# A graph layer's neighbour sum on one core: engine orders written out by hand, two-part float32r rows of 2 KB, and sets of three groups

## The chip, the core and the metric

The kernel runs on one core of a Trainium2 chip. A core has five engines with queues of their own: TensorE (PE, matrix products; PEld is its loading of weights), VectorE (DVE), ScalarE (ACT), GpSimd (POOL) and SyncE (SP). DMA transfers are issued from the queues of POOL, ACT and SP. The metric is the device time of one execution in microseconds (us). Each number of the profile comes from one execution under the hardware profiler.

## What is computed

x has 12500 rows of 256 values, float32. There are 200000 edges with random `src` and sorted `dst`.

```python
h   = relu(layernorm(x))                         # per row
agg = segment_sum(h[src], dst, num_segments=12500)
z   = (1.0 + eps_gin) * h + agg
t   = relu(batchnorm(z @ W1 + b1, g1, bt1))      # W1: 256 x 512
y   = t @ W2 + b2                                # W2: 512 x 256
out = x + relu(batchnorm(y + h, g2, bt2))
```

The batch norms take mean and variance over all 12500 rows, so the first needs every row of `z @ W1`, and the second every row of `y + h`.

## The kernel before

**Tiles.** Nodes are cut into 25 chunks of 512 (`NCH`, `CH`), edges into 1563 tiles of 128, tiles into 131 groups of 12 (`GT`, `NG`). As `dst` is sorted, the edges of a tile reach few nodes; all of a group's nodes lie in a window of `WIDE` = 128 + 2 x `MARGIN` = 280 nodes that moves by `STEP` = 96 nodes per group. A look at the indices ahead (flag L207) picks `fast()` or a general way; with these inputs it is `fast()`.

**A group's work (stage 1).** `gather` (L378 to L387) issues 12 indirect DMAs on POOL (L383), each of which fetches 128 rows by the indices in `srcT` into a buffer `gt`. The pool of these buffers has `AHEAD + 1` = 5, and the loop issues the gather of group i + 4 while it works on group i, so that it needs the buffer of group i - 1. `sums` (L404) makes 12 one-hot matrices of 128 x 128 in one VectorE instruction (L408) and has TensorE multiply and add up the 12 tiles in PSUM (L418): sums by place in a tile's node range. `join` (L423) copies the sums to SBUF on ScalarE (`zs`, L425) and makes the placing matrix `at` (L427); `put` (L432) multiplies both (`pz`, L437), which turns the sums and moves them to their place in the window; `add` (L442) adds the window to the chunk(s) of z that it touches (`zc`, L450). A chunk of z is loaded by `z_chunk` from `h_cols`, the transposed h, and scaled by 1 + eps (L397). When the window has passed a chunk, `first_layer` (L453) multiplies it by W1 in four slices of 128 outputs (L459), takes each slice's statistics (L463) and a copy (L464), and stores all four by one DMA of 1 MB (L465) into `t_tab`.

**The lead-in.** h is made from x by `h_chunk` (L355): `settle` (L323) takes statistics on VectorE (bn_stats L329, over two rows at once), the root on ScalarE (L334), the reciprocal (L336) and the offset (L338) on VectorE, and four relus on ScalarE (L340); the chunk is stored in the table `h_tab` (ACT's queue), transposed on TensorE (L366), copied (L370 on ScalarE, L372 on VectorE) and stored in `h_cols` (SP's queue, L373). Until the table is complete, gathers can't read it. So the first `LEAD` = 24 groups fetch rows of x itself, and `settle` makes h of them in place: 6 bn_stats and 12 relus for a group. `h_chunk` runs in the same iterations.

**Stages 2 and 3** (L510 to L559) read `t_tab` and `h_cols`, multiply by W2, keep `y + h` in SBUF, and after the second statistics transpose back, add x and store.

**What sets the order.** A planner in the language's library orders each engine's instructions; the written order is only a guide to it. In the trace of before it puts, for example, two matmuls of the next group's `sums` ahead of a group's `pz`. Waits between engines follow from the data and the buffers.

Of the kernel before, what the change touches and what calls it, by code (L numbers as in the profile page):

```python
# [7 lines left out]
F32 = mybir.dt.float32  # L8
I32 = mybir.dt.int32
AF = mybir.ActivationFunctionType  # L10
OP = mybir.AluOpType
# [4 lines left out]
R = 4  # L16
EPS = 1e-5
GT = 12
MARGIN = 76
AHEAD = 4  # L20
LEAD = 24
# [9 lines left out]
def kernel(  # L31
# [233 lines left out]
    def fast():  # L265
# [24 lines left out]
        with ExitStack() as fs:  # L290
# [7 lines left out]

            with ExitStack() as es:
                ln = es.enter_context(tc.tile_pool(name="ln", bufs=2))  # L300
                gat = es.enter_context(tc.tile_pool(name="gat", bufs=AHEAD + 1))
                sel = es.enter_context(tc.tile_pool(name="sel", bufs=2))
                zcp = es.enter_context(tc.tile_pool(name="zc", bufs=4))
                tsp = es.enter_context(tc.tile_pool(name="ts", bufs=2))
                ps_h = es.enter_context(tc.tile_pool(name="ps_h", bufs=1, space=PSUM))
                ps_i = es.enter_context(tc.tile_pool(name="ps_i", bufs=1, space=PSUM))
                ps_s = es.enter_context(tc.tile_pool(name="ps_s", bufs=2, space=PSUM))
                ps_z = es.enter_context(tc.tile_pool(name="ps_z", bufs=1, space=PSUM))
                ps_t = es.enter_context(tc.tile_pool(name="ps_t2", bufs=2, space=PSUM))
# [3 lines left out]
                col = ps_i.tile([P, WIDE], F32, name="col")  # L313
# [30 lines left out]
                xts = {}  # L344

                def x_chunk(g):
                    if g >= NCH:
                        return
                    n = chunks[g][1] * R
                    xts[g] = ln.tile([P, R, D], F32, name="xt", bufs=4)  # L350
                    if n < CH:
                        nc.vector.memset(xts[g], 0.0)
                    carry(nc.sync, xts[g], x, g, store=False)

                def h_chunk(g):  # L355
                    n = chunks[g][1] * R
                    slots = len(parts[g])
                    x_chunk(g + 2)
                    ht = ln.tile([P, R, D], F32, name="ht")
                    settle(xts.pop(g), -(-slots // 2), slots, ht, "c")  # L360
                    carry(nc.scalar, ht, h_tab, g, store=True)
                    hc = ln.tile([P, DC, CH], F32, name="hc")
                    for d in range(DC):
                        ph = ps_h.tile([P, CH], F32, name="pc")
                        for c in range(slots):
                            nc.tensor.transpose(  # L366
                                ph[:, c * P : (c + 1) * P], ht[:, c, d * P : (d + 1) * P], ident
                            )
                        if d % 2:
                            nc.scalar.copy(hc[:, d, :n], ph[:, :n])  # L370
                        else:
                            nc.vector.tensor_copy(hc[:, d, :n], ph[:, :n])  # L372
                    nc.sync.dma_start(h_cols[g, :, :, :n], hc[:, :, :n])  # L373

                groups = [(t0, min(GT, NTILE - t0)) for t0 in range(0, NTILE, GT)]
                gathered = {}

                def gather(i):  # L378
                    t0, n = groups[i]
                    ga = gat.tile([P, GT, D], F32, name="gt")  # L380
                    for t in reversed(range(t0, t0 + n)):
                        rows = left if t == full_tiles else P
                        nc.gpsimd.indirect_dma_start(  # L383
                            out=ga[:rows, t - t0, :], out_offset=None, in_=x if i < LEAD else h_tab,
                            in_offset=bass.IndirectOffsetOnAxis(ap=srcT[:rows, t : t + 1], axis=0),
                        )
                    gathered[i] = ga  # L387

                zc = {}

                def z_chunk(c):
                    if c in zc or c >= NCH:
                        return
                    n = chunks[c][1] * R
                    zc[c] = zcp.tile([P, DC, CH], F32, name="zc")
                    nc.sync.dma_start(zc[c][:, :, :n], h_cols[c, :, :, :n])
                    nc.scalar.activation(zc[c][:, :, :n], zc[c][:, :, :n], AF.Copy, scale=gin1)  # L397
# [4 lines left out]
                summed, placed = {}, {}  # L402

                def sums(i):  # L404

                    t0, n = groups[i]
                    oh = sel.tile([P, GT, P], F32, name="oh")
                    nc.vector.tensor_tensor(  # L408
                        oh[:, :n, :],
                        col[:, :P].unsqueeze(1).to_broadcast([P, n, P]),  # L410
                        dstT[:, t0 : t0 + n].unsqueeze(2).to_broadcast([P, n, P]),
                        op=OP.is_equal,
                    )
                    ga = gathered.pop(i)
                    ps = ps_s.tile([P, D], F32, name="ps")
                    for j in range(n):
                        rows = left if t0 + j == full_tiles else P
                        nc.tensor.matmul(  # L418
                            ps, lhsT=oh[:rows, j, :], rhs=ga[:rows, j, :], start=(j == 0), stop=(j == n - 1)
                        )  # L420
                    summed[i] = ps

                def join(i):  # L423
                    zs = sel.tile([P, D], F32, name="zs", bufs=3)
                    nc.scalar.copy(zs, summed.pop(i))  # L425
                    at = sel.tile([P, WIDE], F32, name="at")
                    nc.vector.tensor_scalar(  # L427
                        at, col, shift[:, i : i + 1], None, op0=OP.is_equal
                    )
                    placed[i] = zs, at  # L430

                def put(i):  # L432

                    zs, at = placed.pop(i)
                    pz = ps_z.tile([P, DC, CH], F32, name="pz2")
                    for d in range(DC):
                        nc.tensor.matmul(  # L437
                            pz[:, d, :WIDE], lhsT=zs[:, d * P : (d + 1) * P], rhs=at, start=True, stop=True
                        )
                    return pz  # L440

                def add(i, pz):  # L442
                    lo, hi = span(i)
                    for c in range(max(lo, 0) // CH, -(-min(hi, N) // CH)):
                        z_chunk(c)
                        a, b = max(lo, c * CH, 0), min(hi, (c + 1) * CH, N)
                        if a >= b:
                            continue
                        side = zc[c][:, :, a - c * CH : b - c * CH]
                        nc.vector.tensor_add(side, pz[:, :, a - lo : b - lo], side)  # L450
                    z_chunk(max(lo, 0) // CH + 1)

                def first_layer(c):  # L453
                    n = chunks[c][1] * R
                    ts = tsp.tile([P, HC, CH], F32, name="ts")
                    for f in range(HC):
                        ph = ps_t.tile([P, CH], F32, name="ph")
                        for d in range(DC):
                            nc.tensor.matmul(  # L459
                                ph[:, :n], lhsT=w1s[:, d, f * P : (f + 1) * P],  # L460
                                rhs=zc[c][:, d, :n], start=(d == 0), stop=(d == DC - 1),
                            )
                        nc.vector.bn_stats(st1[:, f, c, :], ph[:, :n])  # L463
                        nc.scalar.copy(ts[:, f, :n], ph[:, :n])  # L464
                    nc.scalar.dma_start(t_tab[c, :, :, :n], ts[:, :, :n])  # L465
                    del zc[c]

                x_chunk(0)
                x_chunk(1)
                for i in range(min(AHEAD, NG)):  # L470
                    gather(i)
                made = done = 0
                for i in range(NG + 1):

                    while made < NCH and made < 2 + NCH * i // (LEAD - AHEAD):
                        h_chunk(made)
                        made += 1
                    if i + AHEAD < NG:
                        gather(i + AHEAD)
                    pz = None  # L480
                    if i > 0:
                        join(i - 1)
                        pz = put(i - 1)
                    if i < NG:
                        if i < LEAD:
                            settle(gathered[i], GT // 2, GT, gathered[i], "g")
                        sums(i)
                    if i == 0:
                        continue
                    add(i - 1, pz)  # L490
                    nxt = span(i)[0] if i < NG else N
                    while done < NCH and min((done + 1) * CH, N) <= nxt:
                        first_layer(done)
                        done += 1
# [316 lines left out]
```

## Time and profile before

| what | value |
|---|---|
| median of 3 runs | 2267.43 us (2265.9 to 2267.68) |
| the profiled execution | 2627.44 us |
| its span, first to last instruction | 2625.6 us |
| its mean granted TensorE clock | 0.754 |
| lead-in with gathers of x, 32 to 505 us | POOL 273.97 us busy, DVE 210.53, ACT 218.53, PE 226.22; DMA share 0.55 |
| gathers of the table, 505 to 2328 us | POOL 1208.69, DVE 372.33, ACT 125.46, PE 922.82; DMA share 0.36 |
| to the start of stage 2, 2328 to 2378 us | PE 37.18, POOL 0 |
| stage 2, 2378 to 2548 us | PE 170.00 |
| stage 3, 2548 to 2626 us | PE 40.86; DMA share 0.77 |

The profiled execution is 360 us longer than the median; all rows below the second are of it. A line of the profile's groups has line, engine, operation, out<-in by the program's names and a count; then busy time in all and the mean of one in ns; then the idle time of the engine just before these instructions, with what ended most of it. "issue" is idle time in which the engine waited for nothing that the profile shows, "remote" a release that it can't tie to an instruction of this core. A line of the waits has who waited for whom, us in all, how often, the longest. A line of the timeline has start, duration, engine, line, operation, and in brackets the idle time before it.

### The profile page before, as it was taken

To read this page: it belongs to the slowest core of one execution; us is meant where nothing else is said; L and a number is where in the kernel's file an instruction comes from. 1 tells how busy PE (TensorE), PEld (TensorE's weight loads), DVE (VectorE), ACT (ScalarE), POOL (GpSimd) and SP (SyncE) were. 2 spreads that over 40 slices of the span, in tenths; PEclk is the share of its full clock that TensorE was granted. 3 is DMA by queue.
4 is the path that set the end of the run, shared out by engine and by line. 5 is a ranking of instruction groups with operands and counts; after the bars stand their busy time and mean duration, and the time that the engine had idled before them with its cause. 6 is when DMAs were issued, how large, how long until landed. Compare 5 with 4: busy or idle time off the path is not lost.

```text
span 2625.6 us, 14777 instructions
## 1 busy us (share of the span) xinstructions
PE 1404.3 (53%) x4873; PEld 1001.2 (38%) x4873; DVE 716.2 (27%) x1060; ACT 460.3 (18%) x871; POOL 1484.3 (57%) x1575
## 2 busy tenths in 40 slices
PE   1234566645455455445545545544555553578995
PEld 1223344434434334343333424433334442453444
DVE  5234555412212112122111212211121211133444
ACT  1335465510000000000000000000000000013434
POOL 4654656666666666666666666566666666630000
PEclk6666777777777777677777767777777776788996
DMA  5444665433333333333333333333333333328728
GB/s 163 158 152 136 206 199 185 139 114 92 116 119 108 100 120 112 92 116 119 113 92 116 112 94 118 105 120 92 119 110 96 116 114 90 108 77 328 273 82 301
DMA packets 150067, 349.41 MB, mean 133 GB/s; under 512 B 28920, under 2 KB 84366, under 8 KB 143838
## 3 DMA queue, kind: packets, MB, share of 16 engines
q0 software_dynamic: 75008, 204.90, 26.9%
q1 hardware_dynamic: 44182, 91.21, 10.0%
q10 hardware_dynamic: 30792, 52.26, 5.3%
q8 instruction: 41, 0.67, 0.1%
q14 instruction: 44, 0.36, 0.0%
HBM read 284.26 MB, written 64.00 MB: 133 GB/s over the span
## 4 chain that ended last, share of the span: by engine, by line
another core or an unknown queue 50%; PE 25%; issue 10%; ACT 6%; DVE 5%; DMA 3%; POOL 1%; ACTq 0%; SPq 0%; DVEq 0%; POOLq 0%
PE ps L418 9%; PE py L527 6%; PE pz L437 4%; PE ph L459 4%; ACT gt L340 3%; DVE st L463 1%; DMA out_dram<-ot 1%; ACT zs L425 1%; POOL gt L383 1%; ACT ht L340 1%; DVE oh L408 1%; PE po L551 1%; ACT zc L397 1%; DMA zc<-h_cols 1%
## 5 line engine op out<-in xcount | busy, mean ns | idle before, releaser
L383 POOL DMA_INDIRECT gt<-h_tab,srcT x1275 | 1208.9, 948 | 616.4 <-issue 373.8
L418 PE MATMUL ps<-gt,oh 128*128 128x256 f32 x3126 | 767.2, 406 | 88.8 <-ACT gt L340 70.8
L418 PEld LDWEIGHTS ps<-gt,oh 128*128 128x128 f32 x3126 | 648.3, 208 | 206.9 <-ACT gt L340 74.3
L437 PE MATMUL pz<-at,zs 128*128 128x280 f32 x524 | 210.8, 538 | 789.1 <-ACT zs L425 672.0
L408 DVE TENSOR_TENSOR oh<-col,dstT 128x1536 f32<-128x1536 f32 x131 | 229.1, 1749 | 1192.6 <-remote 942.9
L437 PEld LDWEIGHTS pz<-at,zs 128*128 128x128 f32 x524 | 121.6, 248 | 850.2 <-ACT zs L425 693.3
L383 POOL DMA_INDIRECT gt<-in_x_dram,srcT x288 | 273.8, 951 | 196.5 <-ACT zs L425 109.3
L425 ACT COPY zs<-ps 128x256 f32<-128x256 f32 x131 | 48.8, 372 | 1614.0 <-remote 1261.3
L459 PE MATMUL ph<-zc,w1s 128*128 128x512 f32 (+1 forms) x400 | 210.3, 677 | 206.2 <-ACT ts L464 138.2
L459 PEld LDWEIGHTS ph<-zc,w1s 128*128 128x128 f32 x400 | 84.9, 220 | 311.6 <-issue 154.9
L450 DVE TENSOR_TENSOR zc<-pz,zc 128x560 f32<-128x560 f32 (+9 forms) x203 | 100.9, 527 | 315.8 <-remote 189.8
L527 PE MATMUL py<-tT,w2s 128*128 128x512 f32 (+1 forms) x400 | 170.9, 591 | 11.7 <-ACT tT L520 11.7
L340 ACT ACTIVATE gt<-gt,nbg,rsg 128x256 f32<-128x256 f32 x288 | 149.5, 590 | 4.2 <-DVE nbg L338 1.9
L527 PEld LDWEIGHTS py<-tT,w2s 128*128 128x128 f32 x400 | 76.9, 193 | 105.7 <-issue 87.2
L463 DVE BATCH_NORM_STATS2 st<-ph 128x6 f32<-128x512 f32 (+1 forms) x100 | 67.1, 681 | 153.5 <-PE ph L459 60.1
L329 DVE BATCH_NORM_STATS2 stg<-gt 128x6 f32<-128x512 f32 x144 | 91.5, 689 | 34.7 <-DMA gt<-in_x_dram,srcT 22.6
L464 ACT COPY ts<-ph 128x512 f32<-128x512 f32 (+1 forms) x100 | 57.4, 575 | 194.9 <-DVE st L463 150.6
L520 ACT ACTIVATE tT<-ti,of,sc 128x512 f32<-128x512 f32 (+1 forms) x100 | 72.1, 791 | 100.8 <-issue 86.7
L366 PE MATMUL pc<-ident,ht 128*128 128x128 f32 x196 | 38.2, 327 | 66.1 <-issue 27.9
L427 DVE TENSOR_SCALAR at<-col,shift 128x280 f32<-128x280 f32 x131 | 65.5, 500 | 0.3 <-PE pz L437 0.3
L531 DVE TENSOR_TENSOR yT<-py,yT 128x512 f32<-128x512 f32 (+1 forms) x50 | 33.9, 678 | 110.2 <-PE py L527 110.2
L366 PEld LDWEIGHTS pc<-ident,ht 128*128 128x128 f32 x196 | 27.7, 168 | 84.9 <-issue 33.8
(74 smaller groups left out, 393.8 us busy)
## 6 DMA issues: line engine op xcount, KB each, us to landing
t_tab<-ts ACTq DMA_DIRECT2D x24, 1024.0 KB
ti<-t_tab SPq DMA_DIRECT2D x24, 1024.0 KB
gt<-h_tab,srcT POOLq DMA_INDIRECT x1275
xt<-in_x_dram SPq DMA_DIRECT2D x24, 512.0 KB
h_tab<-ht ACTq DMA_DIRECT2D x24, 512.0 KB
h_cols<-hc SPq DMA_DIRECT2D x24, 512.0 KB
zc<-h_cols SPq DMA_DIRECT2D x24, 512.0 KB
yT<-h_cols SPq DMA_DIRECT2D x24, 512.0 KB
```

What stands on the lines that cost most here:

```text
L329: nc.vector.bn_stats(st[:, c : c + 2, :].rearrange("p c s -> p (c s)"), v[:, c : c + 2, :].rearrange("p c d -> p d c"),)
L340: nc.scalar.activation(to[:, c, :], v[:, c, :], AF.Relu, bias=nb[:, c : c + 1], scale=rs[:, c : c + 1])
L383: nc.gpsimd.indirect_dma_start(out=ga[:rows, t - t0, :], out_offset=None, in_=x if i < LEAD else h_tab, in_offset=bass.IndirectOffsetOnAxi ...
L408: nc.vector.tensor_tensor(oh[:, :n, :], col[:, :P].unsqueeze(1).to_broadcast([P, n, P]), dstT[:, t0 : t0 + n].unsqueeze(2).to_broadcast([P ...
L418: nc.tensor.matmul(ps, lhsT=oh[:rows, j, :], rhs=ga[:rows, j, :], start=(j == 0), stop=(j == n - 1))
L425: nc.scalar.copy(zs, summed.pop(i))
L437: nc.tensor.matmul(pz[:, d, :WIDE], lhsT=zs[:, d * P : (d + 1) * P], rhs=at, start=True, stop=True)
L450: nc.vector.tensor_add(side, pz[:, :, a - lo : b - lo], side)
L459: nc.tensor.matmul(ph[:, :n], lhsT=w1s[:, d, f * P : (f + 1) * P], rhs=zc[c][:, d, :n], start=(d == 0), stop=(d == DC - 1),)
L463: nc.vector.bn_stats(st1[:, f, c, :], ph[:, :n])
L520: nc.scalar.activation(tT[:, f, :n], ti[:, f, :n], AF.Relu, bias=of1[:, f : f + 1], scale=sc1[:, f : f + 1],)
L527: nc.tensor.matmul(py[:, :n], lhsT=w2s[:, f, d * P : (d + 1) * P], rhs=tT[:, f, :n], start=(f == 0), stop=(f == HC - 1),)
```

## The change

- The planner is switched off for stage 1 (`manual_schedule`): each engine works in the order in which the program is written.
- The table `h_two` takes the place of `h_tab` in `fast()`: a row has 2 x 256 values, the upper part of h (rounded to float32r by a ScalarE copy) and what is left (`lo`, a VectorE subtraction). A gather of it fetches rows of 2 KB.
- `sums` of table groups multiply float32r by float32r with 512 columns (both parts at once); `hold` adds both halves: ScalarE copies one, VectorE adds the other.
- `LEAD` 24 to 30, `AHEAD` 4 to 5, `MARGIN` 76 to 64 (`WIDE` 256). Lead-in gathers have six buffers. Table gathers have five (`LOTS`): two of them in the space of the layernorm pool, three in that of the lead-in buffers. So the first gather of the table comes after `ln.close()`.
- Each lead-in iteration makes one chunk of the table (the first 25 do), then settles group i + 1, multiplies group i, transposes the chunk of the iteration before, places group i - 2, adds group i - 4 and does at most one slice of the first layer.
- After the lead-in the loop goes by sets of three groups: hold, put and add of the three groups of the set before, one-hots of this set, up to three slices of the first layer, then the matmuls of this set, and after each group's matmuls the gather five groups on.
- Each slice of the first layer is stored by a DMA of its own (256 KB).

```diff
-MARGIN = 76
-AHEAD = 4
-LEAD = 24
+MARGIN = 64
+AHEAD = 5
+SET = 3
+LEAD = 30
...
+            h_two = dram.tile([N, 2 * D], F32, name="h_two")
...
+                es.enter_context(tc.manual_schedule())
...
+                LOTS = 5
...
+                lnp = ln.enter_context(tc.tile_pool(name="ln", bufs=2, side="right"))
...
+                lgp = lead.enter_context(tc.tile_pool(name="lg", bufs=6))
...
+                def h_chunk(g):
+
+                    n = len(parts[g])
+                    hts[g] = ht = lnp.tile([P, R, D], F32, name="ht", bufs=3)
+                    settle(xts.pop(g), -(-n // 2), n, ht, "c")
+                    hl = lnp.tile([P, R, 2, D], F32R, name="hl")
+                    hi, lo = hl[:, :n, 0, :], hl[:, :n, 1, :]
+                    nc.scalar.copy(hi, ht[:, :n, :])
+                    nc.vector.tensor_tensor(lo, ht[:, :n, :], hi.bitcast(F32), op=OP.subtract)
+                    carry(
+                        nc.scalar, hl.rearrange("p c s d -> p c (s d)").bitcast(F32), h_two, g, store=True,
+                    )
+                    x_chunk(g + 3)
...
+                    if i < LEAD:
+                        gathered[i] = ga = lgp.tile([P, GT, D], F32, name="gx")
+                    else:
+                        k = (i - LEAD) % LOTS
+                        gathered[i] = pools[k >= 2].tile([P, GT, 2 * D], F32R, name=f"gt{k >= 2:d}")
+                        ga = gathered[i].bitcast(F32)
...
+                def hold(i):
+                    zss[i] = sel.tile([P, D], F32, name="zs", bufs=SET)
+                    if i < LEAD:
+                        nc.scalar.copy(zss[i], bank(i))
+                    else:
+                        nc.scalar.copy(zss[i], bank(i)[:, D:])
+                        nc.vector.tensor_add(zss[i], bank(i)[:, :D], zss[i])
...
+                def take(c, f):
+                    n = chunks[c][1] * R
+                    ph = slices.pop((c, f))
+                    nc.vector.bn_stats(st1[:, f, c, :], ph[:, :n])
+                    ts = tsp.tile([P, CH], F32, name="ts")
+                    nc.scalar.copy(ts[:, :n], ph[:, :n])
+                    nc.scalar.dma_start(t_tab[c, :, f, :n], ts[:, :n])
...
+                for i in range(LEAD):
+                    if i + AHEAD < LEAD:
                         gather(i + AHEAD)
+                    elif i > NCH:
+
+                        if not pools:
+                            ln.close()
+                            pools.append(es.enter_context(
+                                tc.tile_pool(name="ga", bufs=2, side="right", reuse_waits="tile")
+                            ))
+                        if main < LEAD + 2:
+                            gather(main)
+                            main += 1
+                    if i > 3:
+                        add(i - 4)
+                        done["add"] += 1
+                    for c, f in taken:
+                        take(c, f)
+                    if i > 1:
+                        spots(i - 2)
+                        hold(i - 2)
+                    edges(i + 1)
+                    if i < NCH:
+                        h_chunk(i)
+                    if i + 1 < LEAD:
+                        settle(gathered[i + 1], GT // 2, GT, gathered[i + 1], "g")
+                    scale()
+                    sums(i)
+                    if 0 < i <= NCH:
+                        turn(i - 1)
+                    if i > 1:
+                        put(i - 2)
...
+                for i0 in range(LEAD, NG + SET, SET):
...
+                    for i in before:
+                        hold(i)
+                    scale()
+                    ahead = here[i0 == LEAD :]
+                    for k, i in enumerate(before):
+                        put(i)
+                        add(i)
+                        done["add"] += 1
+                        if k:
+                            for j in ahead[:1]:
+                                edges(j)
+                            ahead = ahead[1:]
+                            for c, f in some[:1]:
+                                slice_of(c, f)
+                                take(c, f)
+                            some = some[1:]
...
+                    for i in here:
                         sums(i)
+                        gather(i + LOTS)
```

`turn` is the second half of the former `h_chunk` (transposes, copies, the store to `h_cols`), `edges` the one-hot of `sums`, `spots` the placing matrix of `join`, and `slice_of` the two matmuls of one slice.

## The prediction, made before the changed kernel was run

> **What bounds the kernel now.** I began with busy shares (PE 53%, POOL 57%: nothing is full), went to the costliest groups, then to the waits.
>
> ```profile
> L383 POOL DMA_INDIRECT gt<-h_tab,srcT x1275 | 1208.9, 948 | 616.4 <-issue 373.8
> L418 PE MATMUL ps<-gt,oh 128*128 128x256 f32 x3126 | 767.2, 406 | 88.8 <-ACT gt L340 70.8
> ...
> L383 POOL DMA_INDIRECT gt<-in_x_dram,srcT x288 | 273.8, 951 | 196.5 <-ACT zs L425 109.3
> ```
>
> POOL issues 1275 + 288 = 1563 row gathers at 0.95 us. The timeline around 1600 us shows their rhythm, and its break:
>
> ```profile
> 1611.03 0.95 POOL L383 DMA_INDIRECT gt<-h_tab,srcT  x1 [0.30 <-issue]
> 1612.28 0.95 POOL L383 DMA_INDIRECT gt<-h_tab,srcT  x1 [0.31 <-issue]
> 1613.54 0.95 POOL L383 DMA_INDIRECT gt<-h_tab,srcT  x1 [0.30 <-issue]
> 1618.63 0.37 ACT L425 COPY zs<-ps 128x256 f32<-128x256 f32 x1 [26.13 <-remote]
> 1618.63 1.76 DVE L408 TENSOR_TENSOR oh<-col,dstT 128x1536 f32<-128x1536 f32 x1 [22.82 <-remote]
> 1618.86 0.95 POOL L383 DMA_INDIRECT gt<-h_tab,srcT  x1 [4.38 <-remote]
> ```
>
> Unbroken, starts are 0.949 + 0.304 = 1.2534 us apart: 15.04 us for a group of 12. The break at 1614 is a wait for the buffer of sums three groups back. PE had ended those matmuls near 1598, yet ACT, DVE and POOL go on together at 1618.6. The waits say how much of this reaches POOL:
>
> ```profile
> ACT zs L425 <- remote: 1261.3, 72, 38.9
> DVE oh L408 <- remote: 942.9, 71, 22.8
> ...
> POOL gt L383 <- issue: 456.2, 1487, 2.5
> POOL gt L383 <- remote: 211.7, 50, 6.4
> ...
> POOL gt L383 <- ACT zs L425: 114.1, 14, 19.2
> ```
>
> The "issue" row is the 0.30 us gap. The other two, with some 10 us of small ones, are POOL's real stalls: 336 us. Against the trace's own sum: last gather ends at 2327.9, first starts at 32.4; 1563 x 1.2534 = 1959 us, and 2327.9 - 32.4 - 1959 = 336.
>
> The profiled execution took 2627.4 us (span 2625.6 + 1.8 around it), 360 more than the median of 2267.4. Take away the 336 us and, of the 49.6 us between the last gather and stage 2, the some 20 us of backlog: 2627.4 - 336 - 20 = 2271. That is within 4 us of the median. So I read the plain kernel as POOL's cadence without stalls, and the late releases as mostly belonging to the profiled execution. Its parts: 33 head + 1959 gathers + about 28 to stage 2 + 248 (stages 2 and 3, 2377.5 to 2625.6) + 2 = 2270.
>
> **The change part by part** (durations are means from the groups view with shapes kept apart, pitches from the timeline)
>
> Gather count: unchanged, 1563. LEAD 30 moves 6 x 12 = 72 of them from table rows to rows of x (951 against 948 ns): nothing.
>
> Rows of 2 KB for the other 131 x 12 - 9 - 360 = 1203: not in the trace. Nearest row: this gather with 1 KB. It still names 128 rows. Low bound 0 (cost goes by rows), high bound double (cost goes by bytes), 1203 x 0.949 = 1142 us; below nothing isn't possible with as many rows. The Trainium skill ("DMA: Bandwidth & Descriptors", section on the anatomy of one SWDGE DMA) speaks against the change: its fit is a fixed 2.0 us plus bytes at 436 GB/s, with a dispatch of some 50 ns. By that fit the additional 131 KB are 0.30 us each, 1203 x 0.30 = 362 us if transfers couldn't overlap. The row: POOL lets go of a gather after 0.949 us, min 901, max 963, while a transfer ends about 1.45 us later and others have begun; DMA engines are at 0.36 in 505 to 2328 us. Doubled gather bytes bring that to about 0.65. I take 0 on POOL; the page's dispatch of 50 ns is not what limits (1563 x 0.05 = 78 us against 1959 measured).
>
> Sums: before, 24 records of 0.216 us, 5.2 us a group at full clock. With 512 columns in float32r there is no row: between a quarter of the fp32 512-column matmul (L459, 0.429 us pitch, two records) and the same as that, 2.6 to 10.3 us a group. All below 15.04: beside the gathers, 0 on the path. If POOL's cover were gone, the upper end would still not be last.
>
> Waiting a set later (hold, put, add, slices after the next set starts): a gather waits for sums five groups back, 5 x 15.04 - 15 = about 60 us of room, before about 45. It takes out of the profiled run its 336 us; of the plain run, in my reading, nothing. One-hots for three groups (3 x 1.76 us DVE), the hi/lo add (about 0.37), the copy (0.37): 10 us a set of 45, hidden.
>
> Lead-in, where I see the price. Before, the planner interleaves; per group ACT has about 10.9 us (12 relus 6.1, a chunk's 4 relus 2.1, copies and sqrts 2.7) and DVE about 10.3 (8 bn_stats 5.1, one-hot 1.76, placing 0.5, add 0.75, hc copy 0.7, first layer and small ones 1.5), below 15.04. Now each engine's order is fixed and one iteration makes one chunk, then layernorms group i+1. In the written order ACT and DVE hand over to each other: after the 12 relus of a group come, on ACT, hc copy 0.583, slice copy 0.585, zs copy 0.372, sqrt 0.29, (DVE reciprocal and nb 0.33), 4 relus 2.07, copy of the hi half about 1.0 (from L464: 0.585 for 512 elements, L397: 1.145 for 1024); then DVE's subtraction of 1024 elements 1.17 (L110: 1.796 for 1572), *behind which* the group's 6 bn_stats of 0.69 are queued (3.8 at their pitch), sqrt 0.30, reciprocal and nb 0.37, 12 relus 6.1 (pitch 0.505), a share of the scale 0.23, hand-overs 0.5. Sum 17.7 us, against 15.04. DVE's one-hot, add, table bn_stats lie beside the relus.
>
> Iteration 0 starts near 60 us (group 0 has landed at 49.5, is settled first). 25 iterations of 17.7 end at about 503; the last transpose and h_cols store about 10 later, and gather 30 takes its buffer from that space: 513. POOL would be there at 33 + 360 x 1.2534 = 484. Stall: about 30 us, bounds 0 (if ACT and DVE overlap more, iteration 16.5) and 60 (19 us). It isn't got back, since POOL is the bound. Iterations 25 to 29 have no chunk (some 8.5 us each), so gathers 31 to 34 don't wait. The h_two stores (512 KB instead of 256, ACT's queue) and slice stores (256 KB each) have DMA room (0.55 in 32 to 505).
>
> A second rule against the change: "SBUF — State Buffer", section on the two separate sides of SBUF: DVE in its two-port modes keeps GpSimd from writing descriptors. By that rule the 25 subtractions cost POOL up to 25 x 1.17 = 29 us. The row: two-input fp32 L110 runs 1.14 ns per element, and gathers beside one-hot work are never over 963 ns, but for the first. I take 0.
>
> End: before, about 18 us from the last landing to the end of the first layer. After: two holds and puts, 5 slices, then 4 of chunk 24, each slice some 1.7 PE + 0.69 DVE + copy, about 24: +6. Stages 2 and 3 are untouched.
>
> Sum: 2267.4 + 30 + 6 = 2303, say 2300; own range 2285 to 2325.
>
> **The rivals**
>
> *A, likeliest, 46%: cadence-bound, the lead-in's handovers starve POOL:* 2300.
>
> *B, 15%: same bound, and the lead-in keeps up* (PE, ACT and DVE each below 15 us in sum speak for it; the queue order against): 2263 to 2280.
>
> *C, 14%: 2-KB rows lengthen the gather* on POOL. For it: a row of 2 KB was never run. Against: 0.949 is flat whatever else moves. Each 2% of 1.2534 us is 30 us; up to 2700 at a third more.
>
> *D, other side, 25%: late releases are real.* If the plain run had the same 336 us of stalls, its cadence would have to be (1959 - 336)/1563 = 1.04 us, thus the 0.30 us gap mostly the profiler's. Then a longer buffer chain and work a set later remove the stalls: 33 + 1624 + 107 (lead-in at 514 against POOL at 407) + 34 + 250 = 2048; with half of each, cadence 1.146, 2175. For it: an isolated gap of 0.30 us whose source the profile doesn't show, and lateness that appears only while gathers run (0.04 us after 2332). Against: the sum without stalls meets the median within 4 us. It decides from the point at which the plain cadence is under 1.22 us: each gather of the main part (1203) must give 0.03 us to pay for A's 36 us.
>
> **How the numbers follow.** About 0.2% (4.5 us) is what a measurement can tell from no change. Faster: D and 1 of B, 0.26. Same: 10 of B, 0.10. Slower: A, C and 4 of B, 0.64. Range: all of A and B, C up to 3% (2340), D down to 2110 (16 of 25): 8 in 10. Likeliest 2300.
>
> **What would show it.** Right: gathers 1.25 us apart throughout the changed trace; a hole of 20 to 40 us in POOL before gather 30, ended by the lead-in's last transposes; lead-in iterations near 18 us, the longest step being bn_stats behind the subtraction; next to no POOL stalls after it, so that the profiled execution falls near the median. Wrong: a gather of 2 KB longer than 0.96 us or stalls in the main part (C); no hole (B); a median below 2255, which the profiled cadence can't give (D).

## The result and the profile after

The changed kernel takes 2293.16 us (median of 4 runs, 2292.39 to 2293.38), before 2267.55 (4 runs, 2265.9 to 2269.61): ratio 1.0112, 95% interval 1.0094 to 1.0129. It is slower by 25.6 us; 2300 had been forecast. At times TensorE's releases come late on a chip while gathers run, and then every kernel of this case takes some 2580 to 2670 us (so did the profiled execution of before, and so did the runs that are marked "late" below), so each run stands beside runs of before on the same chip.

The changed kernel's profiled execution has a span of 2290.3 us, 2.1 below its time. Its groups first (line, engine, operation, out<-in, count; busy us, mean ns; idle us before, with what ended it):

```profile
L415 POOL DMA_INDIRECT gt<-h_two,srcT x1203 | 1137.0, 945 | 377.5 <-issue 346.6
L460 PE MATMUL pss<-gt,ohs 128*128 128x512 f32 x1203 | 478.0, 573 | 742.9 <-DMA gt<-h_two,srcT 727.6
...
L415 POOL DMA_INDIRECT gx<-in_x_dram,srcT x360 | 355.7, 988 | 109.8 <-issue 103.4
```

A gather of 2-KB rows takes POOL 945 ns, the gather of 1-KB rows of the table took 948: bytes cost POOL nothing. But the 1-KB gathers of x have gone from 951 to 988 ns, and 360 x 0.037 is 13 us. The waits (us in all, times, longest) show what else POOL lost:

```profile
POOL gt L415 <- issue: 346.6, 1138, 0.3
...
ACT sdg L348 <- DVE stg L343: 135.5, 29, 5.9
...
POOL gx L415 <- issue: 103.4, 339, 0.4
...
DVE hl L376 <- ACT hl L375: 72.6, 23, 3.2
...
POOL gt L415 <- ACT zs L467: 11.4, 1, 11.4
```

The "remote" waits of before are gone, and POOL has one wait of its own left, 11.4 us, once. ScalarE's root of a group (L348) waits 135.5 us in all for the group's statistics, up to 5.9 each time. From the starts of all 1563 gathers: they are 1.250 us apart, but for 18 longer steps that add 26.5 us. One of them is the wait (11.1 us more than the usual gap of 0.3); 17 are long gathers. The timeline shows such a gather (start, duration, engine, line):

```profile
111.24 1.04 ACT L375 CAST hl<-ht 128x1024 fp32r<-128x1024 f32 x1
...
112.32 1.23 DVE L376 TENSOR_TENSOR hl<-ht,hl 128x1024 fp32r<-128x1024 f32 x1 [3.22 <-ACT hl L375]
112.37 1.99 POOL L415 DMA_INDIRECT gx<-in_x_dram,srcT  x1 [0.30 <-issue]
113.46 3.70 DVE L343 BATCH_NORM_STATS2 stg<-gx 128x6 f32<-128x512 f32 x6
113.58 0.37 ACTq L288 DMA_DIRECT2D h_two<-hl  x1
114.67 0.94 POOL L415 DMA_INDIRECT gx<-in_x_dram,srcT  x1 [0.30 <-issue]
```

The gather that starts beside the new subtraction (L376) takes 1.99 us instead of 0.95. 16 of the 17 long gathers lie beside one of the 25 subtractions; the 17th is the first of all, beside a subtraction of the set-up (L112). Together they are 15.3 us over 0.947 each, 13.6 of it beside the 25 subtractions. The same lines show the second thing: VectorE waits 3.22 us for ScalarE's copy of the upper half, and only then starts the six bn_stats of the next group. And this is the hole:

```profile
526.31 0.95 POOL L415 DMA_INDIRECT gt<-h_two,srcT  x1 [0.30 <-issue]
...
530.98 6.92 PE L460 MATMUL pss<-gx,ohs 128*128 128x256 f32 x24 [4.33 <-ACT zs L467]
...
537.93 0.65 ACT L467 COPY zs<-pss 128x256 f32<-128x256 f32 x2 [7.01 <-PE pss L460]
538.64 0.94 POOL L415 DMA_INDIRECT gt<-h_two,srcT  x1 [11.38 <-ACT zs L467]
```

POOL stops after gather 31, until the sums of group 29, the last of the lead-in, have ended at 537.9 (the profile names the copy of these sums, which ends just before POOL starts). The built program says why: the first buffer of the second kind, which gather 32 takes, lies over two lead-in buffers, those of group 24 and of group 29. Gather 30, which I had expected to be held, started at 497.6, without a wait.

### The profile page after: what moved, and what is told of

Its sections match the earlier page's. It is cut to its first block, busy times and chain, and to the rows that moved or that the text cites. A ratio compares the mean times of both kernels' runs of the same rounds, so it can differ in the third digit from the quotient of the medians.

```text
span 2290.3 us, 12738 instructions
## 1 busy us (share of the span) xinstructions
PE 1243.0 (54%) x3670; PEld 833.4 (36%) x3670; DVE 784.2 (34%) x1218; ACT 522.9 (23%) x974; POOL 1494.4 (65%) x1575
## 3 DMA queue, kind: packets, MB, share of 16 engines
q1 hardware_dynamic: 44182, 91.21, 11.4%
## 5 line engine op out<-in xcount | busy, mean ns | idle before, releaser
L415 POOL DMA_INDIRECT gt<-h_two,srcT x1203 | 1137.0, 945 | 377.5 <-issue 346.6
L460 PE MATMUL pss<-gt,ohs 128*128 128x512 f32 x1203 | 478.0, 573 | 742.9 <-DMA gt<-h_two,srcT 727.6
L460 PEld LDWEIGHTS pss<-gt,ohs 128*128 128x128 f32 x1203 | 343.5, 295 | 882.1 <-issue 743.2
L415 POOL DMA_INDIRECT gx<-in_x_dram,srcT x360 | 355.7, 988 | 109.8 <-issue 103.4
L460 PE MATMUL pss<-gx,ohs 128*128 128x256 f32 x720 | 227.9, 490 | 198.9 <-ACT zs L467 160.8
L460 PEld LDWEIGHTS pss<-gx,ohs 128*128 128x128 f32 x720 | 180.5, 256 | 252.6 <-ACT zs L467 178.7
L442 DVE TENSOR_TENSOR ohs<-col,dstT 128x1536 fp32r<-128x1536 f32 x131 | 226.8, 1739 | 0.0
L354 ACT ACTIVATE gx<-gx,nbg,rsg 128x256 f32<-128x256 f32 x360 | 180.1, 587 | 15.0 <-DVE nbg L352 15.0
L481 PE MATMUL pz<-at,zs 128*128 128x256 f32 x524 | 135.7, 393 | 31.4 <-DVE zs L470 31.3
L343 DVE BATCH_NORM_STATS2 stg<-gx 128x6 f32<-128x512 f32 x180 | 111.6, 687 | 11.3 <-DMA gx<-in_x_dram,srcT 11.3
```

The source lines that it names most:

```text
L343: nc.vector.bn_stats(st[:, c : c + 2, :].rearrange("p c s -> p (c s)"), v[:, c : c + 2, :].rearrange("p c d -> p d c"),)
L354: nc.scalar.activation(to[:, c, :], v[:, c, :], AF.Relu, bias=nb[:, c : c + 1], scale=rs[:, c : c + 1])
L415: nc.gpsimd.indirect_dma_start(out=ga[:rows, t - t0, :], out_offset=None, in_=x if i < LEAD else h_two, in_offset=bass.IndirectOffsetOnAxi ...
L442: nc.vector.tensor_tensor(ohs[:, i % SET, :n, :], col[:, :P].unsqueeze(1).to_broadcast([P, n, P]), dstT[:, t0 : t0 + n].unsqueeze(2).to_br ...
L460: nc.tensor.matmul(bank(i), lhsT=oh[:rows, j, :], rhs=ga[:rows, j, :], start=(j == 0), stop=(j == n - 1))
L481: nc.tensor.matmul(pz[:, d, :], lhsT=zs[:, d * P : (d + 1) * P], rhs=at, start=True, stop=True)
```

## The experiments

**More buffers for the kernel before (e5_six_ahead): is the cadence the bound?**

```diff
-AHEAD = 4
+AHEAD = 6
```

> The kernel before with AHEAD = 6, so seven gather buffers instead of five, nothing else. On a chip where it takes 2267: theory 1 (POOL's cadence without stalls bounds it) 2267 within 4 us; rival D (late releases are part of its time) 2175 or less. On a chip where it takes 2600: if TensorE's releases come late by some 20 us whatever POOL does, two more groups of room (30 us) cover them and the time falls to about 2280; if they come only once POOL has run out of work and stops, more buffers only lengthen the lateness, and it stays near 2600.

Measured: 2274.98 us against 2270.21, ratio 1.0021 (1.0013 to 1.0028). No gain, rather 5 us of loss (from the last gather to stage 2 it takes 39.1 us; e8 below, with the buffers of before, 34.6), and its profiled execution (2275.9) has no late release:

```profile
ACT zs L425 <- PE ps L418: 1348.5, 120, 17.1
...
POOL gt L383 <- issue: 468.5, 1537, 0.4
```

All of POOL's idle time is the gap of 0.30 between gathers; steps over 1.2534 us add 1.0 us in all, and the last gather starts at 1987.0, where the prediction's sum had put its end at 1992. Rival D falls: here the plain kernel has no late release, the pace is 1.251 us all the same, and more room gives nothing. That the lateness belongs to profiled executions, as I wrote, falls too: this one was profiled and shows none.

**Each half of POOL's loss taken away.** The edits: e1 writes the lo half on ScalarE (so it holds h, and the remainder is left out), e2 moves buffers, e3 does both.

```diff
-                    nc.vector.tensor_tensor(lo, ht[:, :n, :], hi.bitcast(F32), op=OP.subtract)
+                    nc.scalar.copy(lo, ht[:, :n, :])
```

```diff
-                        gathered[i] = ga = lgp.tile([P, GT, D], F32, name="gx")
+                        gathered[i] = ga = lgp.tile([P, GT, D], F32, name=f"gx{i % 6}", bufs=1)
...
-                        gathered[i] = pools[k >= 2].tile([P, GT, 2 * D], F32R, name=f"gt{k >= 2:d}")
+                        gathered[i] = pools[k >= 2].tile(
+                            [P, GT, 2 * D], F32R, name=f"gt{k >= 2:d}{k if k >= 2 else ''}", bufs=1 if k >= 2 else None
+                        )
```

With the second edit gather 32 lies over the buffers of groups 24 and 25, 33 over 26 and 27, 34 over 28 and 29.

> The lo half of the table is written by a second ScalarE copy instead of the VectorE subtraction (so it holds h and not the remainder; the output isn't the reference's). Theory 1 (the lead-in's hand-overs between ScalarE and VectorE set when sums of group 29 end, and gather 32 waits for that): the stretched gathers (14.9 us) go, but POOL only waits longer before gather 32; the ScalarE copy is 0.19 us shorter than the subtraction and spares a hand-over, 25 times, so about 5 to 8 us less: 2286. Theory 2 (POOL's losses add up, 15 us of stretched gathers and 11 us of waiting): 2278. If neither matters: 2293.

> Only the place of the buffers changes: the first buffer of the second kind lies over those of groups 24 and 25, not over 24 and 29, so that gather 32 no longer waits for the sums of group 29. Theory 1 and 2: the hole of 11.4 us before gather 32 goes, the stretched gathers stay: 2282, with at most a small hole before gather 34. If the hole is only a symptom and POOL is held elsewhere afterwards: 2293.

> Both edits: lo half by a ScalarE copy (it holds h, the output isn't the reference's) and buffers placed so that gather 32 waits for groups 24 and 25 only. Theory 1: with the stretched gathers gone POOL is some 15 us earlier, and now no wait for the lead-in holds it: 26 us less than the changed kernel, 2267, the time of before. Theory 2: also 2267. If the end of the lead-in holds the later gathers in any case (gather 34 needs group 29): 2275 or more.

> The table holds the upper half only, its rows are 1 KB, and the sums have 256 columns (the remainder is left out of the sums, the subtraction is still done). If a gather's time on POOL goes by its 128 rows, not by bytes: 2293 within 3 us, gathers 1.25 us apart as with 2 KB. If 2 KB rows cost POOL anything, less than 2293 by 1203 times that: 1% of 1.25 us would be 15 us.

All four were measured late, beside a before of 2601.2 us. Their ratios, in the order above: 1.0250 (1.0189 to 1.0310), 1.0106 (1.0071 to 1.0142), 1.0177 (1.0118 to 1.0236), 1.0190 (1.0129 to 1.0251). In each trace late releases add over 330 us to POOL's steps, so they tell nothing of 25 us; the same four edits follow once more, under names that end in b.

> The buffer placement alone (gather 32 over the buffers of groups 24 and 25), again, to be read on a chip where the kernel before takes some 2270. Theories 1 and 2: 11 us less than the changed kernel, so about 1.006 of the kernel before (some 2283); the stretched gathers (about 15 us) stay in its trace, the hole before gather 32 is gone. If the hole only moves to a later gather: 1.011, no gain.

Measured: 2281.56 against 2268.61, ratio 1.0058 (1.0045 to 1.0071), without one of its six runs, which took 2567.8 us; no trace of that run exists, so its cause stays open. As expected: 11.6 us less than the changed kernel (each one's before differs by 1 us). In its trace no gather waits more than 0.3 us, and the 17 long gathers are all there (15.1 us):

```profile
L417 POOL DMA_INDIRECT gt<-h_two,srcT x1203 | 1138.1, 946 | 366.5 <-issue 345.8 <-DMA gt<-h_two,srcT 19.2 <-PE ph L501 1.2
L417 POOL DMA_INDIRECT gx<-in_x_dram,srcT x360 | 355.8, 988 | 109.8 <-issue 102.8 <-ACT gx L354 1.8 <-DMA gx<-in_x_dram,srcT 0.9
```

> Placement and the lo half by a ScalarE copy (it holds h; the output isn't the reference's), again. Theory 1: neither stretched gathers nor hole; the ratio to the kernel before falls to 0.997 to 1.002 (2263 to 2274). If the lead-in's end holds later gathers in any case: 1.005 or more.

Measured: 2268.07 against 2268.61, ratio 1.0000 (0.9991 to 1.0008). Without both, the changed kernel has the time of before; one gather of its trace is long, the first.

> The lo half by a ScalarE copy alone (it holds h; the output isn't the reference's), buffers as in the changed kernel, again. Theory 1 (gather 32 waits for the sums of group 29, which the lead-in's chain sets): the stretched gathers go (15 us), the hole before gather 32 grows from 11 to some 20 us, 5 to 8 us less than the changed kernel: ratio to before 1.008 to 1.009. Theory 2 (POOL's losses add up): 15 us less, ratio 1.0045.

Measured: 2268.40 against 2268.59, ratio 0.9997 (0.9989 to 1.0006). Both theories are wrong in size: the one edit takes away all 25 us, the hole as well. The trace tells what I had not priced. These are one chunk's turn in its timeline, and one of its waits:

```profile
119.84 2.51 DVE L343 BATCH_NORM_STATS2 stg<-gx 128x6 f32<-128x512 f32 x4
119.96 2.08 ACT L354 ACTIVATE ht<-xt,nbc,rsc 128x256 f32<-128x256 f32 x4 [0.44 <-DVE nbc L352]
...
122.06 1.04 ACT L375 CAST hl<-ht 128x1024 fp32r<-128x1024 f32 x1
...
123.02 1.04 ACT L376 CAST hl<-ht 128x1024 fp32r<-128x1024 f32 x1
...
DVE stg L343 <- DMA gx<-in_x_dram,srcT: 77.7, 47, 6.4
```

The group's bn_stats now begin with the chunk's relus, not after the subtraction that waits for them and for the copy. ScalarE's wait for the group's statistics falls from 135.5 to 73.8 us, and the root of group 29 starts at 486.0 instead of 522.9. The bn_stats now wait for gathered rows instead (77.7 us in all; 11.3 in the changed kernel): the lead-in keeps up with POOL. So it ends 37 us earlier, and gather 32 finds group 29 done. My expectation had counted only the 0.19 us by which the one instruction is shorter than the other, and a hand-over saved. The mechanism of theory 1 holds, its size here does not.

**Rows of 1 KB (e6_rows_1k_b):** the table holds only the upper half, the sums have 256 columns. Its buffers are half as large too, and `hold` is one ScalarE copy, without VectorE's addition.

```diff
-            h_two = dram.tile([N, 2 * D], F32, name="h_two")
+            h_two = dram.tile([N, D], F32, name="h_two")
...
-                        nc.scalar, hl.rearrange("p c s d -> p c (s d)").bitcast(F32), h_two, g, store=True,
+                        nc.scalar, hl[:, :, 0, :].bitcast(F32), h_two, g, store=True,
...
-                    return pss[:, i % SET, :D] if i < LEAD else pss[:, i % SET, :]
+                    return pss[:, i % SET, :D]
```

> Rows of 1 KB (the upper half only; the remainder is left out of the sums), again. If POOL's time goes by rows: the time of the changed kernel within 3 us, ratio to before 1.010 to 1.0125, gathers 1.25 us apart as with 2 KB. If bytes cost: below 1.005.

Measured: 2275.26 against 2268.59, ratio 1.0027 (1.0018 to 1.0036): 18 us less than the changed kernel, which looks like the rival. The trace says it is not. A row of 1 KB costs POOL what one of 2 KB costs:

```profile
L415 POOL DMA_INDIRECT gt<-h_two,srcT x1203: 902/949/963, 496.3 to 2001.6; - x172
```

(min/median/max ns, first and last start; the changed kernel has 903/946/962, 497.6 to 2010.8.) With smaller buffers gather 32 lies over group 24 alone, so the hole is gone as in e2_pair_b, where the last gather starts at 2000.8; that is 9.2 of the 18 us. Most of the rest is the end: from the last gather's start to stage 2's first matmul 25.1 us, against 31.8. The two-part form costs nothing on POOL, but some 7 us after it; which of rows, columns and the addition of halves takes them was not tried.

**Subtractions put into the kernel before (e4_before_sub):**

```diff
                     settle(xts.pop(g), -(-slots // 2), slots, ht, "c")
+                    lo = ln.tile([P, R, D], F32, name="lo")
+                    for _ in range(4):
+                        nc.vector.tensor_tensor(lo[:, :slots, :], ht[:, :slots, :], ht[:, :slots, :], op=OP.subtract)
```

> The kernel before, with four VectorE subtractions of two SBUF tiles (1024 float32 each, the result is used by nothing) after each chunk's layernorm: 100 in all, beside the gathers of the lead-in. If such a subtraction holds off the gather that starts beside it (0.6 us on average in the changed kernel's trace): 40 to 100 us more, 2310 to 2370. If the stretched gathers were only chance or cost nothing: 2268, VectorE has the room.

Measured: 2313.90 against 2268.59, ratio 1.0196 (1.0182 to 1.0210): 45.3 us for 100 subtractions. In its trace 77 gathers take over 1.0 us, 45.9 us over 0.947 in all; 76 of them lie beside one of the 100 subtractions, the other is the first of all:

```profile
L386 POOL DMA_INDIRECT gt<-h_tab,srcT x1275 | 1205.3, 945 | 388.3 <-issue 385.3 <-PE ph L462 1.8 <-DMA gt<-h_tab,srcT 0.9
L386 POOL DMA_INDIRECT gt<-in_x_dram,srcT x288 | 318.5, 1106 | 87.9 <-issue 83.3 <-ACT gt L340 1.2 <-DMA gt<-in_x_dram,srcT 0.9
```

288 x (1.106 - 0.947) = 45.8 us, within a microsecond what the kernel lost; the table's gathers, with no subtraction beside them, stay at 945 ns. This also shows again that POOL's time is the kernel's time. VectorE had room for the work.

**The subtraction moved, not removed (e9_sub_later):** behind the next group's statistics.

```diff
-                        h_chunk(i)
+                    rest = h_chunk(i) if i < NCH else None
                     if i + 1 < LEAD:
                         settle(gathered[i + 1], GT // 2, GT, gathered[i + 1], "g")
+                    if rest:
+                        rest()
```

(`rest` does the subtraction and the store of the chunk.)

> The changed kernel with one step moved: the VectorE subtraction (and the store of the table chunk that waits for it) stands behind the next group's statistics, reciprocal and offset instead of ahead of them; nothing else. If the lead-in's pace of 16.9 us comes from the 6 bn_stats queued behind the subtraction: pace 15 to 15.5, no hole before gather 32, and the stretched gathers stay (25 subtractions, 10 to 20 us): ratio to before 1.003 to 1.007. If the pace comes from ScalarE's own sum or from hand-overs elsewhere: 16 us or more, the hole stays, ratio 1.010 to 1.012. If the subtraction's place also decides how many gathers it meets: below 1.003.

Measured late: 2643.72 against 2613.07, ratio 1.0108 (1.0076 to 1.0140). It settles nothing. What can be read is only that the steps from one group's root to the next, while chunks are made, go down to 12.2 us, where in the late e2_pair none is under 15.3. That the order alone would end the lead-in in time stays open.

**Stage 2 in float32r, on the kernel before (e8_stage2_f32r):** t and W2 are rounded to it, and `XAHEAD` is 9, for room.

```diff
+                w2r = tsb.tile([P, HC, D], F32R, name="w2r", bufs=1)
+                nc.vector.tensor_copy(w2r, w2s)
...
-                    tT = tsb.tile([P, HC, CH], F32, name="tT")
+                    tT = tsb.tile([P, HC, CH], F32R, name="tT")
...
-                                py[:, :n], lhsT=w2s[:, f, d * P : (d + 1) * P], rhs=tT[:, f, :n],
+                                py[:, :n], lhsT=w2r[:, f, d * P : (d + 1) * P], rhs=tT[:, f, :n],
```

> The kernel before, with stage 2 multiplied in float32r (t and W2 rounded to it; 9 instead of 10 buffers for x in stage 3). Stage 2 is TensorE's, 170 us at 100%. If a float32r matmul of 512 columns takes half of a float32 one or less, DMA (share 0.64 of 170: 109 us) bounds it: some 55 us less, 2213. If it takes as long: 2268.

Measured: 2188.24 against 2268.59, ratio 0.9644 (0.9631 to 0.9657), 80 us less, where 55 had been expected, and the fastest of all. The windows (busy us and count of PE, PEld, DVE, ACT, POOL; granted clock, DMA share, GB/s) give the end of stage 1, stage 2 and stage 3:

```profile
1985.00:2020.00 35.00, 22.42 (x74) 14.59 (x74) 10.33 (x23) 5.28 (x12) 1.30 (x2) 0.84 0.46 172
2020.00:2108.00 88.00, 70.55 (x200) 33.41 (x200) 59.51 (x97) 71.09 (x100) 0.00 (x0) 0.94 1.02 408
2108.00:2187.00 79.00, 40.12 (x196) 36.91 (x196) 33.71 (x38) 36.07 (x51) 0.00 (x0) 0.68 0.89 304
```

Stage 2 goes from 170 to 88 us. DMA's share there is 1.02, and no engine is busy for more than 71.1 of the 88 us, so I read DMA as its bound now, which was not tried by itself. My 109 us from DMA's former share was too high. The idea came from the change's float32r; it works in stage 2, where TensorE was busy for all of 170 us, and stage 1's sums were not such a place.

## Why the prediction was right, and where it was not

*The bound.* Right: POOL's 1563 gathers at an even pace (1.250 us; 1.2534 forecast), and in before no stall. e5 and e4 show it from both sides. (Before's last gather ends at 2327.6; the prediction's 2327.9 counts the gap behind it.) Wrong beside it: the late releases are not the profiler's, and to work a set later does not take them out (the late traces of e1, e2 and e3). That the changed kernel's profiled execution fell near its median is therefore no sign for the prediction's reading.

*Rows of 2 KB at nothing.* Right on POOL (945 ns; e6), not at the end (some 7 us with the rest of the two-part form). DMA's share while the table is gathered is 0.77 (540 to 2012 us), not 0.65.

*Sums and work a set later: nothing on the path.* Right: after gather 32 no gather waits more than 0.3 us.

*The lead-in: 30 us.* Right in that POOL is starved for the lead-in's hand-overs, with the bn_stats queued behind the subtraction (e1: take the subtraction from VectorE and all of it is gone). Wrong in place and size. While chunks were made the pace was 16.9 us from one hi copy to the next, not 17.7, and gather 30 was not held. Gather 32 was, by the place of its buffer, which I had not looked for, and for 11 us, not 30. The term behind it is "Iterations 25 to 29 have no chunk (some 8.5 us each), so gathers 31 to 34 don't wait": the last four steps from root to root took 8.9, 15.9, 10.2 and 14.0 us. The changed trace shows the last of them:

```profile
516.48 0.70 DVE L510 BATCH_NORM_STATS2 st<-ph 128x6 f32<-128x512 f32 x1 [6.20 <-PE ph L499]
...
519.14 3.70 DVE L343 BATCH_NORM_STATS2 stg<-gx 128x6 f32<-128x512 f32 x6
...
522.87 0.31 ACT L348 ACTIVATE sdg<-stg,epst 128x12 f32<-128x12 f32 x1 [4.31 <-DVE stg L343]
```

VectorE waits 6.20 us for the matmuls of a first-layer slice, with the group's bn_stats queued behind: the same fault of order in another place. With 8.5 us a step, group 29's sums would have ended near 523 (an estimate: 15 us earlier), before gather 32 was due at 527.6.

*"I take 0"* for the rule that VectorE can keep GpSimd from its descriptors. This is the step that failed. Its bound was 29 us; the 25 subtractions cost 13.6 (15.3 with the first gather, which the set-up lengthens in before too). I had weighed it against gathers beside the one-hot work, and that is another kind of instruction: one of its two operands, `col`, is in PSUM, while the subtraction reads both from SBUF. The Trainium skill ("SBUF — State Buffer", section on the two separate sides) names the case beside the two-port modes that I had gone by: a VectorE instruction with two SBUF inputs, against a GpSimd operation that reads SBUF. The trace of before held an instance, which I had passed over as "but for the first":

```profile
31.23 1.80 DVE L110 TENSOR_TENSOR dstT<-dstT,base 128x1572 f32<-128x1572 f32 x1 [0.75 <-DVE flag L207]
...
32.40 1.61 POOL L383 DMA_INDIRECT gt<-in_x_dram,srcT  x1 [0.42 <-issue]
```

The first gather takes 1.61 us, beside a subtraction of two SBUF tiles that ends at 33.03.

*The end: +6.* Wrong in sign. From the last gather's start to stage 2 it is 31.8 us; e8, whose stage 1 is that of before, has 34.6: 3 less. The size is loose, as single traces differ (e1, e2 and e3: 32.1 to 34.4; e5 and e4: 39.1 and 39.6).

*The sum.* 30 + 6 = 36 was forecast. Measured on the same places: the last gather starts at 2010.8 instead of 1985.7 (e8), +25.2, of which the hole is 11.1 and long gathers some 14; the end gives -2.8. Together that is 22.4 of the 25.6 by which the medians differ. Two errors, a stall taken too long and a lock taken as nothing, offset each other. So the number came out partly by luck; the time alone wouldn't have told.

## What to carry to other kernels

When one engine's steady pace is the time, what doesn't hold it up is free up to its last start, and what delays one of its starts is paid in full: look at the durations of its instructions, not only at its waits, since an instruction that is held off from within counts as busy. In an order written by hand, an instruction that waits for another engine delays what is queued behind it; put it behind the work that the next hand-over needs. Space that is used again carries the wait of its latest former owner, so the first new buffer should lie over the earliest freed ones.

## What the runs showed of the hardware that was not expected

A VectorE subtraction of two SBUF tiles of 1024 float32 (1.21 to 1.23 us) holds off a gather that starts during it: 16 of 25 in the changed kernel, 76 long gathers for 100 subtractions in e4, 0.45 us for each subtraction there. All 16 end 0.82 us after the subtraction's end. The other nine subtractions began 0.15 to 0.18 us after a gather had started: that gather took its usual 0.95 us, the subtraction its usual 1.23, and the next gather, 1.07 to 1.11 us into the subtraction, at most 0.97. One-hot instructions of 1.74 us, with one operand in PSUM, did not hold a gather; that the operand's place is the reason was not tried by itself.

A float32r matmul of 512 columns in stage 2 takes 70.5 us / 200 = 0.35 us of TensorE's time, where float32 took 170 / 200 = 0.85.

When releases came late, more room didn't help: with the changed kernel's six lead-in buffers and its work put off by a set, POOL's longer steps added 349 to 379 us (e1, e2, e3 late), with before's 337. What makes them late no run here tells.
